# Loading z and x ahead of most weights, and preparing the weights in steps among the first tiles of z

## The chip, the core and the metric

The kernel runs on one core of one Trainium2 chip. The metric is the device time of one execution, in microseconds (us). Inputs and output lie in the chip's memory (DRAM) at the start and at the end. All arithmetic is in 32-bit floats.

## What is computed

The input `x` is one image of 128 x 256 positions (S = 128 rows, I = 256 places in a row) with C = 256 channels. Two layers follow one another, each with a residual sum:

```
x = x + L0(gn(x), z, ...)      # attention along each row, 8 heads of 32, biased by z
x = x + L1(gn(x), ...)         # attention along each row, 4 heads of 64, within a band of +-16
```

`gn` is a group norm over the whole image: 32 groups of 8 channels, each with one mean and one variance taken over all 128 x 256 positions. Nothing of layer 0 can be normalized before all of `x` has been read once.

Layer 0 turns each row `m` (256 x 256) into queries, keys and values with `Wq`, `Wk`, `Wv` after a layer norm, adds to the scores a bias `b = layer_norm(z) @ Wb.T` (one 256 x 256 matrix for each of the 8 heads, the same for all rows), takes a softmax, weighs the values, gates the result with `sigmoid(m @ Wg.T + bg)` and projects it with `Wo`. `z` is 256 x 256 x 128, so it is 33.6 MB, as large as `x`. Layer 1 projects with `w_in` (3 x 256 columns), takes the banded softmax and projects with `w_out`.

The scale and shift of the layer norms are folded into the weights on the chip before they are used: `wq`, `wk`, `wv` and `wb` are multiplied by the norm's scale, have their column means taken out (with a matrix product by `avg`, a matrix of 1/128), and the norm's shift becomes the biases `qb`, `kb`, `vb_r`, `bz_r`. A few more constants are scaled too (`w_in`, `bin_c`, `bg_c`, `wo`), and the bias of layer 1's values is carried through `w_out` into `bout_r` (with the helper tile `bv_w`). This is called the preparation below.

## The kernel before

`fast_kernel` holds the work that is timed. It has these stages.

1. **Constants.** 26 DMAs, all issued by SyncE (SP in the profile), load the weights and the small vectors (the helpers `load_chunks`, `load_col`, `load_row`, and the loops for `w_out` and `bv_c`), 2.6 MB together. The preparation stands in the text right after the pools are opened (L996 to L1040).
2. **Front.** The 16 tiles of `z` (`zjobs`, 2.1 MB each) and the 8 blocks of `x` (4.2 MB each) are read once. `z_front` loads a tile of z and takes its statistics (16 BATCH_NORM_STATS2 on VectorE, L1069); `z_back` turns the tile of the round before on TensorE (L1091), ScalarE copies it out of PSUM (L1093), and `z_project` multiplies it by `wbz`, a copy of the prepared `wb`; every second tile, a table of exponentials of the bias goes to `eb` (L1135). `x_block` loads a block of x and takes its statistics (16 BATCH_NORM_STATS2 on 512 elements, L1144).
3. **Group norm of layer 0 and first rows.** After the last block of x, `plan` spreads the moments, the loads of the first pairs of rows and their normalization over the remaining tiles of z (`mark` is called four times in each tile).
4. **Layer 0**, 64 pairs of rows, then **layer 1**, 64 pairs of rows, both ordered by hand and mostly bound by TensorE.

The order inside the front is written out by hand (`tc.manual_schedule()` keeps it). In the constants and at the boundary of the layers the framework's scheduler orders each engine. Engines run their own queues in order; a DMA is issued in the order of the queue that issues it.

The loop of the front, before:

```python
for n, job in enumerate(zjobs):
    front = z_front(*job)
    if behind is not None:
        z_back(*behind)
    behind = (*job, *front)
    if nx < nga and nx * 9 <= n * nga:
        x_block(nx)
        nx += 1
        if nx == nga:
            ended = n
    mark(4)
```

So x block 0 goes with tile 0, none goes with tile 1, and blocks 1 to 7 go with tiles 2 to 8; `ended` is 8, and `plan` counts from there. There are three buffers for tiles of z and two for blocks of x: the load of tile n + 3 waits until tile n has been turned, and the load of block j + 2 waits until the statistics of block j are done.

At the boundary of the layers, `moments_steps` finishes the second group norm and writes `M1` and `R1` (`M_l`, `R_l` in the profile, L984; POOL takes the root at L979). Then `bv_w`, `ps_bo` and the sum into `bout_r` (L1614 to L1620), the turning of `M1` and `R1` (`ps_mr`, L1628), the scaling of `w_in` by `R1c` (L1631), and the loads of layer 1's first pairs (`xt1`, L1647), which `turn` transposes (`ps_x`, L1655). The pool that holds `xt1` reuses memory that layer 0 has given back; its first loads wait for whatever used that memory last.

Of the kernel before, what the change touches and what calls it, by code (L numbers as in the profile page):

```python
# [9 lines left out]
F32 = mybir.dt.float32  # L10
AF = mybir.ActivationFunctionType
ALU = mybir.AluOpType
# [4 lines left out]
P = 128  # L17
# [756 lines left out]
def fast_kernel(  # L774
# [25 lines left out]
    nc = tc.nc  # L800
    S, I, C = x.shape
    CZ = z.shape[2]
    H = wbT.shape[1]
# [4 lines left out]
    NB = I // P  # L808
    KC = C // P
# [3 lines left out]
    QS = 1.0 / math.sqrt(D0)  # L813
    QS1 = 1.0 / math.sqrt(D1)

    const = ctx.enter_context(tc.tile_pool(name="const", bufs=1))
# [4 lines left out]
    ones = const.tile([P, P], F32, name="ones")  # L821
    nc.vector.memset(ones, 1.0)
    avg = const.tile([P, P], F32, name="avg")
    nc.vector.memset(avg, 1.0 / P)
    mhalf = const.tile([P, 64], F32, name="mhalf")
    nc.vector.memset(mhalf, -0.5)

    def load_chunks(src, n, name):
        t = const.tile([P, src.shape[0] // P, n], F32, name=name)
        nc.sync.dma_start(t, src.rearrange("(k p) n -> p k n", p=P))  # L830
        return t

    def load_col(src, name):
        t = const.tile([P, src.shape[0] // P], F32, name=name)
        nc.sync.dma_start(t, src.rearrange("(k p) -> p k", p=P))
        return t

    def load_row(src, name):
        n = src.shape[0]
        t = const.tile([P, n], F32, name=name)  # L840
        nc.sync.dma_start(t, src.unsqueeze(0).broadcast_to([P, n]))
        return t


# [63 lines left out]

    eb = const.tile([P, H, NB, I], F32, name="eb")

    wq = load_chunks(wqT, C, "wq")
    wk = load_chunks(wkT, C, "wk")
    wv = load_chunks(wvT, C, "wv")
    wg = load_chunks(wgT, C, "wg")
    wo = load_chunks(woT, C, "wo")
    w_in = load_chunks(w_inT, 3 * C, "w_in")

    w_out = const.tile([P, KC, C], F32, name="w_out")
    for a in range(KC):
        for h in range(H1):  # L920
            n = P // H1
            nc.sync.dma_start(w_out[h * n : (h + 1) * n, a, :], w_outT[(2 * h + a) * n : (2 * h + a + 1) * n, :])
    wb = const.tile([CZ, H], F32, name="wb")
    nc.sync.dma_start(wb, wbT)
    lnw_c = load_col(ln_m_w, "lnw_c")
    lnb_c = load_col(ln_m_b, "lnb_c")
    lzw_c = load_col(ln_z_w, "lzw_c")
    lzb_c = load_col(ln_z_b, "lzb_c")
    bg_c = load_col(bg, "bg_c")
    bin_c = load_col(b_in[0 : 2 * C], "bin_c")  # L930
    bo_r = load_row(bo, "bo_r")
    bv_c = const.tile([P, KC], F32, name="bv_c")
    for h in range(H1):
        n = P // H1
        nc.sync.dma_start(
            bv_c[h * n : (h + 1) * n, :],
            b_in[2 * C + h * D1 : 2 * C + (h + 1) * D1].rearrange("(a i) -> i a", i=n),
        )
    bout_r = load_row(b_out, "bout_r")

    qb = const.tile([P, KC], F32, name="qb")
    kb = const.tile([P, KC], F32, name="kb")
    vb_r = const.tile([P, C], F32, name="vb_r")
    bz_r = const.tile([P, H], F32, name="bz_r")
# [42 lines left out]
    pz = tc.alloc_tile_pool(name="pre_z", bufs=1, side="right")  # L987
# [4 lines left out]
    def mm(name):  # L992
        return ps_mm.tile([P, 512], F32, name=name, tag="mm")


    lnb_w = pz.tile([P, KC, P], F32, name="lnb_w")  # L996
    for k in range(KC):
        nc.vector.tensor_scalar_mul(lnb_w[:, k, :], ones, lnb_c[:, k : k + 1])
    for w, dst in ((wq, qb), (wk, kb)):
        for m in range(KC):  # L1000
            ps = mm("b_ps")
            for k in range(KC):
                nc.tensor.matmul(
                    ps[:, 0:1], w[:, k, m * P : (m + 1) * P], lnb_c[:, k : k + 1],
                    start=(k == 0), stop=(k == KC - 1),
                )
            nc.vector.tensor_copy(dst[:, m : m + 1], ps[:, 0:1])
    nc.vector.tensor_scalar_mul(qb, qb, QS)
    ps = mm("b_ps")
    for k in range(KC):  # L1010
        nc.tensor.matmul(ps[:, :C], lnb_w[:, k, :], wv[:, k, :], start=(k == 0), stop=(k == KC - 1))
    nc.vector.tensor_copy(vb_r, ps[:, :C])
    lzb_w = pz.tile([P, P], F32, name="lzb_w")
    nc.vector.tensor_scalar_mul(lzb_w, ones, lzb_c)
    ps = mm("b_ps")
    nc.tensor.matmul(ps[:, :H], lzb_w, wb, start=True, stop=True)
    nc.vector.tensor_copy(bz_r, ps[:, :H])

    for k in range(KC):
        nc.vector.tensor_scalar(wq[:, k, :], wq[:, k, :], lnw_c[:, k : k + 1], QS, ALU.mult, ALU.mult)  # L1020
        nc.vector.tensor_scalar_mul(wk[:, k, :], wk[:, k, :], lnw_c[:, k : k + 1])
        nc.vector.tensor_scalar_mul(wv[:, k, :], wv[:, k, :], lnw_c[:, k : k + 1])
        nc.vector.tensor_scalar_mul(w_in[:, k, 0:C], w_in[:, k, 0:C], QS1)

    for w in (wq, wk, wv):
        ps = mm("b_ps")
        for k in range(KC):
            nc.tensor.matmul(ps[:, :C], avg, w[:, k, :], start=(k == 0), stop=(k == KC - 1))
        for k in range(KC):
            nc.vector.scalar_tensor_tensor(w[:, k, :], ps[:, :C], -1.0 / KC, w[:, k, :], ALU.mult, ALU.add)  # L1030
    nc.vector.tensor_scalar_mul(wb, wb, lzw_c)
    nc.vector.tensor_scalar_mul(bin_c[:, 0:KC], bin_c[:, 0:KC], QS1)

    nc.vector.tensor_scalar_mul(bg_c, bg_c, 0.5)
    nc.vector.tensor_scalar_mul(wo.rearrange("p k n -> p (k n)"), wo.rearrange("p k n -> p (k n)"), 0.5)


    ps = mm("b_ps")
    nc.tensor.matmul(ps[:, :H], avg, wb, start=True, stop=True)
    nc.vector.tensor_sub(wb, wb, ps[:, :H])  # L1040

    nga = S // GA
    st0 = pz.tile([P, nga, G, 3], F32, name="st0")
# [5 lines left out]
    IB, IS = 32, 64  # L1049
    zjobs = [(b, i) for b in range(NB) for i in range(0, I, IB)]  # L1050
    z_rows = z.rearrange("(u t) (p b) c -> t p u (b c)", t=NB, b=NB)
    wbz = pz.tile([P, 4, 4, H], F32, name="wbz")
    nc.vector.memset(wbz, 0.0)
    for j in range(4):
        nc.vector.tensor_copy(wbz[:, j, j, :], wb)

    def z_front(b, i0):

        nonlocal zrs
        zt = pz.tile([P, IB, CZ], F32, name="zt", tag="zt", bufs=3)  # L1060
        nc.sync.dma_start(
            zt.rearrange("p (u b) c -> p u (b c)", b=NB), z_rows[b, :, i0 // NB : (i0 + IB) // NB, :]
        )

        st = pz.tile([P, IB, 3], F32, name="zst", tag="zst", bufs=2)
        for i in range(0, IB, 2):
            if i % (IB // 4) == 0 and i:
                mark(i // (IB // 4))
            nc.vector.bn_stats(  # L1069
                st[:, i : i + 2, :].rearrange("p i f -> p (i f)"),  # L1070
                zt[:, i : i + 2, :].rearrange("p i c -> p c i"),
            )
        at = i0 % IS
        if at == 0:
            zrs = pz.tile([P, IS], F32, name="zrs", tag="zrs", bufs=3)
        rs = zrs[:, at : at + IB]
        nc.vector.tensor_scalar(rs, st[:, :, 2], 1.0 / CZ, 1e-5, ALU.mult, ALU.add)
        nc.gpsimd.tensor_tensor(rs, rs, mhalf[:, :IB], ALU.pow)
        return zt, zrs
# [383 lines left out]
    ended = None  # L1463

    def mark(quarter):
        if ended is not None:
            plan.pop((n - ended, quarter), nothing)()


    behind, nx, n = None, 0, 0  # L1470
    with tc.manual_schedule():
        for n, job in enumerate(zjobs):
            front = z_front(*job)
            if behind is not None:
                z_back(*behind)
            behind = (*job, *front)
            if nx < nga and nx * 9 <= n * nga:
                x_block(nx)
                nx += 1
                if nx == nga:  # L1480
                    ended = n
            mark(4)
        assert not plan
        z_back(*behind)
        z_project()
        z_exp()
        now.project("qT", 0)
        now.project("kT", 0)
        for f in ("centre", "scale"):
            getattr(nxt, f)()  # L1490
        for r in range(2):
            nxt.moments(r)
# [8 lines left out]
    with tc.manual_schedule():  # L1501
        old = was = Nobody()
        es = nn3 = None
        for p in range(NP):
# [3 lines left out]
            ps = now.scores(0, 0)  # L1508
# [95 lines left out]
    with tc.tile_pool(name="l1", bufs=2) as sb, tc.tile_pool(  # L1604
# [4 lines left out]

        def mm1(name):  # L1610
            return ps_mm.tile([P, 512], F32, name=name, tag="mm")


        bv_w = const.tile([P, KC, P], F32, name="bv_w")  # L1614
        for k in range(KC):
            nc.vector.tensor_scalar_mul(bv_w[:, k, :], ones, bv_c[:, k : k + 1])
        ps = mm1("ps_bo")
        for k in range(KC):
            nc.tensor.matmul(ps[:, :C], bv_w[:, k, :], w_out[:, k, :], start=(k == 0), stop=(k == KC - 1))
        nc.vector.tensor_add(bout_r, bout_r, ps[:, :C])  # L1620


        nM1 = const.tile([P, KC], F32, name="nM1")
# [292 lines left out]
```

## Time and profile before

| | us |
|---|---|
| median of 5 runs (3374.55 to 3379.31) | 3375.36 |
| the profiled execution, its own time | 3375.4 |
| its span, first to last instruction (granted TensorE clock 0.982) | 3373.6 |
| first load of z issued | 17.4 |
| statistics of the last block of x begin | 155.3 |
| first scores of layer 0 | 242.6 |
| `R_l` of the second group norm written | 2119.3 |
| first transpose of layer 1 | 2123.9 |

The times below are microseconds from the start of the span. PE is TensorE, PEld its weight loads, DVE VectorE, ACT ScalarE, POOL GpSimd, SPq and ACTq the issuing of DMAs by SyncE and ScalarE. In a line of the timeline stand the start, the duration, the engine, the line of the code, the operation, what it writes and reads, how many instructions are merged, and in brackets how long the engine had been idle before and what released it. A line of the windows gives for one stretch the busy time of each engine, the granted TensorE clock, the busy share of the 16 DMA engines and what they moved.

### The profile page before, as it was taken

Reading aid. Unit: us, or ns where it says so; the run is one execution under the profiler, and the core shown is the slowest. Engines: PE = TensorE matmul, PEld = TensorE weight load, DVE = VectorE, ACT = ScalarE, POOL = GpSimd, SP = SyncE. Lnnn points to the kernel's source line nnn. Section 1 sums busy time; section 2 is a strip of 40 time slices with the busy share of each in tenths; the row PEclk is TensorE's granted clock in tenths of the full one; section 3 lists DMA queues with packets and bytes.
Section 4 is the critical chain, followed back from the end, with each engine's and each line's share of the span. In section 5 each row is a group of like instructions: output and inputs, shape, how many; then the busy total and the mean of one; then the engine's idle time right before and its main releaser. Section 6 shows DMA issues by size and latency. Waiting matters only on the chain. (4 is left out here: it accounts for less than half of the span.)

```text
span 3373.6 us, 81186 instructions
## 1 busy us (share of the span) xinstructions
PE 3226.1 (96%) x35158; PEld 2036.2 (60%) x35158; DVE 2023.4 (60%) x3218; ACT 1463.7 (43%) x2121; POOL 1974.7 (59%) x1377
## 2 busy tenths in 40 slices
PE   5389999999999999999999998899999999999998
PEld 3255555555555555555555554567767767677676
DVE  7966666666666666666666666366544444443456
ACT  2264444444444444444444443344444444444443
POOL 2378887777777777887777774333333333333332
PEclk8699999999999999999999999899999999999999
DMA  9951212221221222122212221121111211212111
GB/s 333 383 135 42 73 48 74 73 73 48 73 74 54 59 71 68 48 73 74 73 48 73 73 65 50 54 64 53 60 57 52 65 52 53 64 52 62 55 57 53
DMA packets 198814, 262.89 MB, mean 78 GB/s; under 512 B 46288, under 2 KB 147536, under 8 KB 197296
## 3 DMA queue, kind: packets, MB, share of 16 engines
q1 hardware_dynamic: 197776, 257.35, 24.9%
q8 instruction: 278, 4.55, 0.7%
q14 instruction: 88, 0.72, 0.1%
q10 hardware_dynamic: 672, 0.26, 0.0%
HBM read 188.82 MB, written 68.75 MB: 76 GB/s over the span
## 5 line engine op out<-in xcount | busy, mean ns | idle before, releaser
L1310 POOL TENSOR_TENSOR eboth<-e 128x512 f32<-128x512 f32 x512 | 640.4, 1273 | 389.7 <-DVE e L1305 386.5
L1305 DVE TENSOR_TENSOR e<-ps_sc,eb 128x1024 f32<-128x1024 f32 x512 | 602.8, 1219 | 316.2 <-ACT ps_sc L1296 225.5
L1296 ACT ACTIVATE ps_sc<-ps_sc 128x1024 f32<-128x1024 f32 x512 | 492.8, 1006 | 507.4 <-PE ps_sc L1289 507.4
L1705 POOL TENSOR_TENSOR e<-e,bw 128x384 f32<-128x384 f32 x256 | 259.8, 1038 | 443.3 <-ACT e L1703 443.3
L1666 PE MATMUL ps_p<-xgT,w_in 128*128 128x512 f32 x1024 | 467.9, 600 | 0.0
L1658 POOL TENSOR_TENSOR xt<-xt,bout_r 128x1024 f32<-128x1024 f32 x64 | 152.3, 2380 | 382.3 <-PE ps_x L1655 382.3
L1758 DVE TENSOR_TENSOR yo<-ps_y,xt 128x512 f32<-128x512 f32 x128 | 88.4, 690 | 380.8 <-PE ps_y L1754 372.5
L1666 PEld LDWEIGHTS ps_p<-xgT,w_in 128*128 128x128 f32 x1024 | 188.4, 190 | 198.9 <-issue 165.4
L1289 PE MATMUL ps_sc<-qT,kT 32*128 32x256 f32 x4096 | 293.7, 400 | 2.1 <-ACT kT L1259 2.1
L1320 PE MATMUL ps_ov<-e,v 128*32 128x256 f32 x4096 | 274.1, 385 | 0.5 <-DVE oT L1334 0.5
L1255 PE MATMUL ps_p<-xnT,wq 128*128 128x512 f32 x512 | 254.1, 618 | 0.7 <-POOL xnT L1242 0.6
L1255 PE MATMUL ps_p<-xgT,wg 128*128 128x512 f32 x512 | 253.9, 618 | 0.0
L1754 PE MATMUL ps_y<-w_out,oT 128*128 128x256 f32 x1024 | 250.3, 387 | 2.6 <-DVE oT L1739 2.6
L1362 PE MATMUL ps_y<-wo,oT 128*128 128x256 f32 x1024 | 243.9, 381 | 7.2 <-POOL oT L1352 7.2
L1362 PEld LDWEIGHTS ps_y<-wo,oT 128*128 128x128 f32 x1024 | 195.7, 191 | 88.3 <-issue 59.5
L1289 PEld LDWEIGHTS ps_sc<-qT,kT 32*128 32x128 f32 x4096 | 185.4, 184 | 94.4 <-issue 70.5
L1270 PE MATMUL ps_v<-wv,xnT 128*128 128x256 f32 x1024 | 242.1, 379 | 0.0
L1255 PE MATMUL ps_p<-xnT,wk 128*128 128x512 f32 x512 | 240.6, 592 | 0.0
L1681 PE MATMUL ps_v<-w_in,xgT 128*128 128x256 f32 x1024 | 231.8, 379 | 0.0
L1736 DVE RECIPROCAL rv<-odd 128x256 f32<-128x256 f32 x128 | 224.4, 1753 | 4.4
L1681 PEld LDWEIGHTS ps_v<-w_in,xgT 128*128 128x128 f32 x1024 | 194.4, 190 | 53.5 <-issue 30.1
L1270 PEld LDWEIGHTS ps_v<-wv,xnT 128*128 128x128 f32 x1024 | 189.6, 190 | 50.9 <-issue 31.1
(163 smaller groups left out, 4986.2 us busy)
## 6 DMA issues: line engine op xcount, KB each, us to landing
zt<-in_z_dram SPq DMA_DIRECT2D x16, 2048.0 KB
xa<-in_x_dram SPq DMA_DIRECT2D x8, 4096.0 KB
xt<-in_x_dram SPq DMA_DIRECT2D x64, 512.0 KB
rvb<-rsum SPq DMA_DIRECT2D x256, 128.0 KB
x<-xo SPq DMA_DIRECT2D x16, 2048.0 KB
xt<-x SPq DMA_DIRECT2D x64, 512.0 KB
out_dram<-yo SPq DMA_DIRECT2D x63, 512.0 KB
rs_r<-rs_d SPq DMA_DIRECT2D x63, 256.0 KB
```

Of the source, the lines that this page charges most:

```text
L1255: nc.tensor.matmul(ps, w[:, k, m * P : (m + 1) * P], getattr(self, src)[:, k, :], start=(k == 0), stop=(k == KC - 1),)
L1270: nc.tensor.matmul(self.ps_v[:, b * C : (b + 1) * C], self.xnT[:, k, t * P : (t + 1) * P], wv[:, k, :], start=(k == 0), stop=(k == KC - 1),)
L1289: nc.tensor.matmul(self.pss[q // 2][:, q % 2, b, :], self.kT[rs, c, r * I + b * P : r * I + (b + 1) * P], self.qT[rs, c, r * I : (r + 1) * I],
L1296: nc.scalar.activation(self.pss[a], self.pss[a], AF.Exp)
L1305: nc.vector.tensor_tensor(e, pss[a], eb[:, h : h + 2], ALU.mult)
L1310: nc.gpsimd.tensor_tensor(t, es[a][:, :, 0, :], es[a][:, :, 1, :], ALU.add)
L1320: nc.tensor.matmul(ov[q * D0 : (q + 1) * D0, :], self.v[:, r, b, h * D0 : (h + 1) * D0], es[q // 2][:, q % 2, b, :], start=(b == 0), stop= ...
L1362: nc.tensor.matmul(self.ps_y[:, b * C : (b + 1) * C], self.oT[r][:, k, b * P : (b + 1) * P], wo[:, k, :], start=(k == 0), stop=(k == KC - 1),)
L1666: nc.tensor.matmul(ps, w_in[:, k, n * C + m * P : n * C + (m + 1) * P], self.xgT[:, k, :], start=(k == 0), stop=(k == KC - 1),)
L1681: nc.tensor.matmul(ps[:, b * C : (b + 1) * C], self.xgT[:, k, t * P : (t + 1) * P], w_in[:, k, 2 * C : 3 * C], start=(k == 0), stop=(k == ...
L1705: nc.gpsimd.tensor_tensor(e[:, q], e[:, q], bcast(bw.rearrange("p b w -> p (b w)"), 1, KC), ALU.mult)
L1754: nc.tensor.matmul(ps[:, b * C : (b + 1) * C], self.oT[r][:, k, b * P : (b + 1) * P], w_out[:, k, :], start=(k == 0), stop=(k == KC - 1),)
```

## The change

- The helpers no longer issue DMAs. They put them on a list, `queued`, and `load(n)` issues the next n of the list from ScalarE's queue.
- The list has a new order: `lnb_c`, `wq`, `wk`, `wv`, `wb`, `lnw_c`, `lzw_c`, `lzb_c` first, then `wg`, `wo`, `w_in`, `w_out` (8 pieces), `bg_c`, `bin_c`, `bo_r`, `bv_c` (4 pieces), `bout_r`.
- The front begins with the load of z tile 0 in two halves (SyncE), the first eight of the list (ScalarE), and the load of z tile 1 (SyncE). From tile 1 on, four of the list are issued from ScalarE after the statistics of each tile, until it is empty (tile 5).
- x block 0 moves from tile 0 to tile 1 (`nx < n`); blocks 1 to 7 stay with tiles 2 to 8, and `ended` stays 8.
- The preparation becomes a generator, `weights()`, that is taken in steps: two steps after tile 0's statistics, three among those of tile 1 (`mark`), one after them, and the rest among tile 6's.
- `bv_w`, `ps_bo` and the sum into `bout_r` move from the boundary of the layers into that last part, and `bv_w` goes from the pool `const` to the pool `pz`.

```diff
+    queued = []
+
+    def load(n):
+        for _ in range(min(n, len(queued))):
+            nc.scalar.dma_start(*queued.pop(0))
+
     def load_chunks(src, n, name):
         t = const.tile([P, src.shape[0] // P, n], F32, name=name)
-        nc.sync.dma_start(t, src.rearrange("(k p) n -> p k n", p=P))
+        queued.append((t, src.rearrange("(k p) n -> p k n", p=P)))
         return t
...
+    def weights():
+        lnb_w = pz.tile([P, KC, P], F32, name="lnb_w")
+        for k in range(KC):
+            nc.vector.tensor_scalar_mul(lnb_w[:, k, :], ones, lnb_c[:, k : k + 1])
+        for w, dst in ((wq, qb), (wk, kb)):
...
+            yield
+            for m in range(KC):
+                nc.vector.tensor_copy(dst[:, m : m + 1], pss[m][:, 0:1])
...
+        nc.vector.memset(wbz, 0.0)
+        for j in range(4):
+            nc.vector.tensor_copy(wbz[:, j, j, :], wb)
+        yield
+        for k in range(KC):
+            nc.vector.tensor_scalar_mul(w_in[:, k, 0:C], w_in[:, k, 0:C], QS1)
...
+        bv_w = pz.tile([P, KC, P], F32, name="bv_w")
...
+        ps = mm("ps_bo")
+        for k in range(KC):
+            nc.tensor.matmul(ps[:, :C], bv_w[:, k, :], w_out[:, k, :], start=(k == 0), stop=(k == KC - 1))
+        yield
+        nc.vector.tensor_add(bout_r, bout_r, ps[:, :C])
...
-    def z_front(b, i0):
+    def z_load(b, i0, parts=1):
+        zt = pz.tile([P, IB, CZ], F32, name="zt", tag="zt", bufs=3)
+        for u in range(parts):
+            part = slice(u * IB // parts, (u + 1) * IB // parts)
+            nc.sync.dma_start(
+                zt[:, part].rearrange("p (u b) c -> p u (b c)", b=NB),
+                z_rows[b, :, (i0 + part.start) // NB : (i0 + part.stop) // NB, :],
+            )
+        return zt
+
+    def z_front(b, i0, zt):
...
     def mark(quarter):
+        if n == 1 and quarter < 4 or n == 6:
+            next(prepare, None)
         if ended is not None:
             plan.pop((n - ended, quarter), nothing)()
...
     behind, nx, n = None, 0, 0
+    prepare = weights()
     with tc.manual_schedule():
+        zts = [z_load(*zjobs[0], 2)]
+        load(8)
+        zts.append(z_load(*zjobs[1]))
         for n, job in enumerate(zjobs):
-            front = z_front(*job)
+            front = z_front(*job, zts.pop(0) if zts else z_load(*job))
+            if n == 0:
+                next(prepare)
+                next(prepare)
+            else:
+                load(4)
+                if n == 1:
+                    next(prepare)
             if behind is not None:
                 z_back(*behind)
             behind = (*job, *front)
-            if nx < nga and nx * 9 <= n * nga:
+            if nx < n and nx < nga:
                 x_block(nx)
...
-        bv_w = const.tile([P, KC, P], F32, name="bv_w")
-        for k in range(KC):
-            nc.vector.tensor_scalar_mul(bv_w[:, k, :], ones, bv_c[:, k : k + 1])
-        ps = mm1("ps_bo")
-        for k in range(KC):
-            nc.tensor.matmul(ps[:, :C], bv_w[:, k, :], w_out[:, k, :], start=(k == 0), stop=(k == KC - 1))
-        nc.vector.tensor_add(bout_r, bout_r, ps[:, :C])
```

## Prediction, made before the changed kernel had run

> **What bounds the kernel now.** I read the windows first, cut where the timelines show the front's stages to change (columns: stretch, length, busy us and instruction count of PE, PEld, DVE, ACT, POOL, granted clock, DMA share, GB/s).
>
> ```profile
> 0.00:17.40 17.40, 3.12 (x15) 3.12 (x15) 2.91 (x18) 1.28 (x1) 2.90 (x15) 1.00 0.50 144
> 17.40:155.30 137.90, 69.97 (x411) 47.41 (x410) 124.82 (x304) 43.38 (x91) 43.76 (x9) 0.76 1.03 389
> 155.30:165.00 9.70, 0.00 (x0) 0.00 (x0) 9.66 (x17) 0.00 (x0) 5.11 (x1) 0.50 1.09 354
> 165.00:179.00 14.00, 8.79 (x56) 6.71 (x56) 11.16 (x37) 4.64 (x9) 6.10 (x2) 0.66 0.16 55
> 179.00:224.00 45.00, 39.41 (x320) 24.98 (x313) 31.60 (x105) 34.36 (x78) 33.96 (x9) 1.00 0.93 252
> ```
>
> For 17.4 us nothing is near its limit. From 17.4 to 155.3 the DMA engines are full (1.03, 389 GB/s) and VectorE is busy 124.8 of 137.9 us: two limits side by side. Then VectorE alone finishes the last block of x; from 165 to 179 the DMA engines run empty, so what follows doesn't depend on how much they had moved before.
>
> The timeline of SyncE's queue says why the first stretch is empty:
>
> ```profile
> 0.80 0.44 SPq L830 DMA_DIRECT2D wq<-in_wqT_dram  x1
> ...
> 16.93 0.42 SPq L841 DMA_DIRECT2D bout_r<-in_b_out_dram  x1
> 17.40 0.43 SPq L1061 DMA_DIRECT2D zt<-in_z_dram  x1
> 17.88 4.25 SPq L1142 DMA_DIRECT2D xa<-in_x_dram  x1
> ```
>
> Twenty-six issues of about 0.5 us stand ahead of the first tile of z. VectorE's timeline tells which limit ends last at the other end:
>
> ```profile
> 117.78 5.41 DVE L1069 BATCH_NORM_STATS2 zst<-zt 128x6 f32<-128x256 f32 x16
> 123.22 0.18 DVE L1077 TENSOR_SCALAR zrs<-zst 128x32 f32<-128x32 f32 x1
> 123.83 9.64 DVE L1144 BATCH_NORM_STATS2 st<-xa 128x6 f32<-128x512 f32 x16 [0.42 <-DMA xa<-in_x_dram]
> ...
> 155.28 9.61 DVE L1144 BATCH_NORM_STATS2 st<-xa 128x6 f32<-128x512 f32 x16 [0.44 <-DMA xa<-in_x_dram]
> ```
>
> Blocks 5 and 7 of x wait 0.4 us for their data: DMA ends last, VectorE half a microsecond behind. Last, the timeline at the boundary of the layers:
>
> ```profile
> 2118.98 0.29 DVE L984 COPY R_l<-rs_l 128x256 f32<-128x256 f32 x1 [5.55 <-POOL rs_l L979]
> ...
> 2119.40 0.93 SPq L1647 DMA_DIRECT2D xt<-x  x2
> ...
> 2119.91 0.15 DVE L1630 COPY R1c<-ps_mr 128x1 f32<-128x1 f32 x1
> ...
> 2123.85 1.94 PE L1655 MATMUL ps_x<-ident,xt 128*128 128x128 f32 x8 [3.51 <-DMA xt<-x]
> ```
>
> Layer 1's first load is issued only after `R_l` is written, and TensorE waits 3.51 us for it. Everything else between 242.6 us and the end isn't touched by the change.
>
> **What the skill says.** The Trainium skill, "DMA: Bandwidth & Descriptors", section "Issuing engines are not separate DMA queues": DMAs from ScalarE and SyncE run on the same 16 engines and interleave; a second issuer saves only issue time. Its section "Queues, rings and completion order" adds that each engine takes turns between queues, packet by packet. The trace agrees: at 200.39 us ScalarE sends `rs_d` just after SyncE issued a tile of z at 200.25; that tile is used first at 216.32, 16.1 us later, where the one before (issued 193.01, used 202.13) took 9.1. So I let weights and z share the bandwidth, and give no bandwidth for the second queue.
>
> **Part 1: the loads.** The stream of z and x is issued from 0.8 us instead of 17.4. Before the last block of x it needs 9 x 2.097 + 8 x 4.194 = 52.4 MB; at 389 GB/s that is 134.8 us, and the trace took 137.9 from first issue to use, so start and landing cost 3.1 us. After the change the weights ride along: five of 0.262 MB, `w_in` 0.786, `w_out` 0.262, two broadcast rows of 0.131, 2.62 MB or 6.7 us. Last block ready: 0.8 + 3.1 + 55.05 MB / 389 GB/s (141.5) = **145.4**, against 155.3. Gain 9.9. The small vectors cost little: `lnb_c`, issued at 12.02, releases VectorE at 14.26, 2.2 us with its latency.
>
> The 26 issues move to ScalarE: 0.5 us each, 13 us. The first twelve stand ahead of its first copy (`zT`), before it has work; the others come four to a tile, 2 us, where ScalarE is busy 43.4 of 137.9 us. Behind them in its queue are the copies that TensorE's transposes wait for, and behind those the next loads of z; room for 2 us is there, as the tile loads are queued some 10 us before they are needed. In the program as built, DMAs share eight semaphores in turn, which adds waits: tile 1 waits until `wv` has landed, `lzb_c` until the first half of tile 0. By the shared rate, `wq`, `wk`, `wv` and as much of z (1.6 MB, 4 us) are there by about 8 us, while the second half of tile 0 flows until 11: no gap. The blocks' waits on small loads (block 1 on `w_in`, block 2 on a piece of `w_out`) end well before SyncE reaches them.
>
> **Part 2: the preparation on VectorE.** It used to lie in the empty stretch; now it lies between statistics. From the rows of the timeline: `lnb_w` 0.48, four copies 0.64, `qb` 0.16, `lzb_w` 0.28, `vb_r` and `bz_r` 0.57, six scalings 2.05, `wb` 0.22, six sums with the column means 2.28, `wb` and `wbz` 0.71: 7.4 us, 0.8 of them while tile 1 is still on its way. At tile 6: `w_in` 0.49, `bin_c` and `bg_c` 0.32, `wo` 0.43, `bv_w` 0.56, `bout_r` 0.41: 2.2 us. Is VectorE then the limit? Tile 1 lands after z0, z1, 0.79 MB of first weights and 1.3 MB of the next, 6.3 MB: 0.8 + 3.1 + 16.2 = 20.1. Its statistics (5.6) with 6.6 of preparation and about 1 us of round trips to TensorE (before, VectorE waited 1.7 and 0.8 us for the column means; now statistics fill most of that) end at 33.3. From x block 0 to block 7 the old trace took 155.28 - 37.82 = 117.5 us, 3.6 of it waiting for x; one tile of z less (5.6) and 2.2 more give 110.5. VectorE reaches block 7 at **143.8**, before the data. The cover of the 9.6 us of new work is thus thin, 1.6 us: every microsecond beyond it shows.
>
> x block 0 moves from tile 0 to tile 1: the order of the stream is z0, z1, x0, z2, x1 instead of z0, x0, z1, z2, x1; no bytes change, and `ended` stays 8. After block 7 the sequence of every engine is the old one, and the DMA engines idle inside it, so the rest of the front moves rigidly with block 7.
>
> **Part 3: the boundary.** `ps_bo` takes TensorE 2.1 us at 2113.5, beside POOL's root (5.44 us), and `bout_r` takes VectorE 0.41 us while it waits for `ps_mr` anyway: their removal brings nothing. But moving `bv_w` out of `const` shifts the buffers of `xt1`. In the changed program the first of these loads waits no longer for `R_l`; it waits for an old `rvb` load, a product of the second last pair and an old projection, and stands in SyncE's queue right behind the store of 2102.21. It is there before 2119. The next thing late is `ps_mr` (about 2120.3 on TensorE) and `R1c` (2120.06), so the transposes start near 2120.3 instead of 2123.85: **3.5**. Neither the transposes nor ScalarE's first copy wait for the last store.
>
> **Sum.** 9.9 + 3.5 = 13.4. The profiled execution took 3375.4 us (span 3373.6 and 1.8 around it), the median is 3375.36, so nothing is to be corrected: **3362.0**. About 0.2% (6.8 us) is what a measurement of this kernel can tell from no change.
>
> Bounds. Part 1 and 2: at least 6 (round trips and shared bandwidth cost VectorE 4 us more at tile 1), at most 14 (the stream at 400 GB/s, as from 80 to 120 us: 3.9 less). Part 3: from 0 to 3.8, as the load is either still late or not; a loss is excluded, because the work there only shrinks.
>
> **Rivals.**
>
> 1. *Both parts as worked out:* 3362.0, from 3358 to 3366. For it: SyncE's lines and the wait of 3.51. Chance 0.62.
> 2. *Another wait takes the load's place at the boundary*, for instance `xt1` shares the engines with the 2.1 MB store of 2102.21 and a store's landing holds a first reuse of memory: only part 1 remains, 3365.5. Against it: 17 us lie between the store and 2119. Chance 0.13.
> 3. *VectorE takes the gain:* the steps of the preparation expose TensorE's round trips and tile 1 comes late by shared bandwidth. If the preparation's 7.4 us and 4 us of waits both show in full, part 1 shrinks from 9.9 to about 3, and the total is 3369, within 0.2% of before. For it: only 1.6 us of cover. Chance 0.10.
> 4. *Slower: ScalarE's queue is held.* SyncE's issue of tile 1 took 15.03 us in the old trace (the longest of that line's sixteen durations), because it was pushed while the engines were full. If an issue from ScalarE is held as long behind SyncE's, its copies, TensorE's transposes and the next loads of z are late at each of tiles 2 to 5. About 10 us of a hold are covered (tile 4's buffer was free some 10 us before its issue at 59.98); the rest shows four times: 4 x 5 = 20 us, less 13.4: 3382. It decides from 10 + 13.4 / 4 = 13.4 us a tile. Against it: ScalarE's issue at 200.39 took 0.40 us, though SyncE wasn't seen to push then. Chance 0.06.
> 5. *The waits for data go too:* with a stream at 400 GB/s and VectorE close behind, 17.4 us come back: 3358. Chance 0.09.
>
> That the change doesn't do what it says would be a late first z after all: its issue has no wait in the program, so I give that nothing beyond case 3.
>
> Range: cases 1, 2 and 5 and most of 3, 3357 to 3369.5. Faster by over 0.2%: cases 1, 2, 5 and a little of 3, 0.86; the same 0.08; slower 0.06.
>
> **What would show it.** Right: z issued at 0.8; tile 0's statistics at 8 to 10 us, tile 1's near 20, block 0's near 33, block 7's near 145 (now 155.28), first scores near 232.7 (now 242.6); 389 GB/s from about 4 us on; the first `ps_x` about 1.4 us after `R_l` instead of 4.9. Wrong: a `zT` copy held by a DMA issue on ScalarE, VectorE waiting for `b_ps` for more than 2 us among tile 1's statistics, block 7 later than 149, or the distance from block 7 to the first scores other than 87.3 us.

## The result, and the profile after

The changed kernel takes 3369.46 us (median of 22 runs, 3367.3 to 3371.64), the kernel before 3376.44 (42 runs). The ratio is 0.998, with a 95% interval from 0.9974 to 0.9985: 7.0 us faster, where 13.4 had been predicted. The profiled executions are 5.5 us apart (spans 3368.1 and 3373.6), and this sum is what the two traces can explain:

| stretch | before | after | gain |
|---|---|---|---|
| start to the statistics of block 7 of x | 155.28 | 151.45 | +3.83 (predicted 9.9) |
| block 7 to the first `e` of layer 0 | 89.59 | 91.38 | -1.79 (predicted 0) |
| first `e` to `R_l` | 1874.11 | 1874.33 | -0.22 |
| `R_l` to the first `ps_x` of layer 1 | 4.87 | 1.19 | +3.68 (predicted 3.5) |
| first `ps_x` to the end | 1249.75 | 1249.75 | 0 |

The boundary came out as predicted, the front gave well under half, and a stretch that was called rigid was 1.8 us longer in these two executions. The timeline around `R_l` shows the first of these:

```profile
2100.87 1.87 SPq L1685 DMA_DIRECT2D xt<-x  x2
...
2117.16 0.29 DVE L990 COPY R_l<-rs_l 128x256 f32<-128x256 f32 x1 [5.55 <-POOL rs_l L985]
...
2118.35 1.94 PE L1693 MATMUL ps_x<-ident,xt 128*128 128x128 f32 x8
```

Layer 1's first load is issued 16 us ahead of `R_l` instead of 0.4 us behind it, and the bracket with the wait for `xt` is gone.

VectorE's timeline of the front (in brackets the idle time before, and what ended it):

```profile
7.90 2.74 DVE L1103 BATCH_NORM_STATS2 zst<-zt 128x6 f32<-128x256 f32 x8 [6.30 <-DMA zt<-in_z_dram]
...
23.35 1.42 DVE L1103 BATCH_NORM_STATS2 zst<-zt 128x6 f32<-128x256 f32 x4 [6.36 <-DMA zt<-in_z_dram]
...
35.13 9.75 DVE L1178 BATCH_NORM_STATS2 st<-xa 128x6 f32<-128x512 f32 x16
...
70.86 9.64 DVE L1178 BATCH_NORM_STATS2 st<-xa 128x6 f32<-128x512 f32 x16 [4.42 <-DMA xa<-in_x_dram]
...
87.22 9.60 DVE L1178 BATCH_NORM_STATS2 st<-xa 128x6 f32<-128x512 f32 x16 [1.19 <-DMA xa<-in_x_dram]
...
151.45 9.60 DVE L1178 BATCH_NORM_STATS2 st<-xa 128x6 f32<-128x512 f32 x16
```

Tile 0 is there at 7.9 us, as predicted. Tile 1 is 3.3 us later than predicted (23.35 against 20.1), blocks 2 and 3 wait 5.6 us, and block 7 starts late and without a wait. The windows say what the stream did meanwhile (last two columns: DMA share and GB/s):

```profile
44.00:48.00 4.00, 2.53 (x24) 1.87 (x24) 4.00 (x12) 1.49 (x4) 0.00 (x0) 1.00 0.86 351
48.00:52.00 4.00, 3.29 (x32) 2.23 (x28) 3.92 (x11) 2.46 (x6) 1.52 (x1) 1.00 0.18 42
52.00:56.00 4.00, 0.98 (x8) 0.07 (x8) 4.00 (x8) 0.75 (x2) 3.90 (x1) 1.00 1.04 358
```

From 48 to 52 us the engines were nearly empty: 42 GB/s. SyncE's waits name the reason (what the issue waited for: us in total, times, longest):

```profile
SPq L1176 <- DMA bv_c<-in_b_in_dram: 18.3, 1, 18.3
SPq L1090 <- DMA xa<-in_x_dram: 17.0, 1, 17.0
...
SPq L1090 <- DMA wv<-in_wvT_dram: 10.8, 1, 10.8
...
SPq L1176 <- DMA w_in<-in_w_inT_dram: 5.7, 1, 5.7
```

The same view of the kernel before, up to 250 us:

```profile
SPq L1142 <- DVE zrs L1077: 88.0, 6, 15.0
SPq L1061 <- PE ps_t L1091: 41.1, 5, 16.1
...
SPq L1184 <- DVE zrs L1077: 14.8, 1, 14.8
SPq L922 <- DMA w_in<-in_w_inT_dram: 2.4, 1, 2.4
```

A load of z (L1090) stood 17.0 us for a load of x, with which it shares no data: in the program as built, tile 3 counts on the same semaphore (the counter by which a finished load is reported) as block 1, and it was issued only at 50.57, when block 1 had landed. Tile 1 stood 10.8 us for `wv`, block 3 long for a piece of `bv_c`. In the kernel before, every wait that showed on the loads of z and x in the front was for a buffer. But waits between loads that share no data were there already, among the weights: a piece of `w_out` (L922) stood 2.4 us for `w_in`.

In the tail of the front, VectorE waits for the last two tiles of z. First the changed kernel, then the kernel before:

```profile
212.31 5.43 DVE L1103 BATCH_NORM_STATS2 zst<-zt 128x6 f32<-128x256 f32 x16 [7.88 <-DMA zt<-in_z_dram]
220.28 5.42 DVE L1103 BATCH_NORM_STATS2 zst<-zt 128x6 f32<-128x256 f32 x16 [2.33 <-DMA zt<-in_z_dram]
```
```profile
216.32 5.43 DVE L1069 BATCH_NORM_STATS2 zst<-zt 128x6 f32<-128x256 f32 x16 [7.73 <-DMA zt<-in_z_dram]
...
222.84 5.43 DVE L1069 BATCH_NORM_STATS2 zst<-zt 128x6 f32<-128x256 f32 x16 [0.86 <-DMA zt<-in_z_dram]
```

The wait of some 8 us for tile 14 was there before the change.

### The profile page after: what moved, and what is told of

Its sections match the earlier page's. It is cut to its first block, busy times and chain, and to the rows that moved or that the text cites. A ratio compares the mean times of both kernels' runs of the same rounds, so it can differ in the third digit from the quotient of the medians.

```text
span 3368.1 us, 81193 instructions
## 1 busy us (share of the span) xinstructions
PE 3219.8 (96%) x35158; PEld 2030.7 (60%) x35158; DVE 2020.8 (60%) x3218; ACT 1462.0 (43%) x2121; POOL 1973.4 (59%) x1377
```

## The experiments

The theory after the result: (a) the boundary's gain comes only from the pool that `bv_w` is taken from, which moves the addresses of the buffers; (b) the front lost to waits on **shared semaphores**, which join loads that have no data in common; (c) the tail depends on how the small send of `rs_d` falls against the last loads of z. The rivals: the work taken from the boundary is what helped there; the stream's bandwidth and VectorE would have set block 7 in any case; TensorE sets the tail.

All results in one table. Each ratio is to runs of the kernel before on the same chip. These runs differ from chip to chip: their medians are 3376.44 beside the changed kernel, 3377.24 beside e1 and e2, 3378.69 beside e3 to e6 and 3376.87 beside e7 to e10. So ratios are compared below, and medians only within one chip. The last three columns are from the one profiled execution of each.

| run | median | ratio (95% interval) | block 7 | block 7 to first `e` | `R_l` to `ps_x` |
|---|---|---|---|---|---|
| before | | | 155.28 | 89.59 | 4.87 |
| changed | 3369.46 | 0.9980 (0.9974 to 0.9985) | 151.45 | 91.38 | 1.19 |
| e1_loads_0_5 | 3367.62 | 0.9973 (0.9962 to 0.9983) | 149.61 | 91.07 | 1.18 |
| e1_loads_0_6 | 3370.57 | 0.9979 (0.9972 to 0.9986) | 151.57 | 90.79 | 1.19 |
| e2_bv_w_in_const | 3373.97 | 0.9992 (0.9983 to 1.0) | 152.04 | 91.33 | 4.77 |
| e2_before_bv_early | 3374.32 | 0.9989 (0.9981 to 0.9998) | 155.82 | 91.89 | 1.19 |
| e3_loads_gpsimd | 3370.57 | 0.9976 (0.9966 to 0.9986) | 150.38 | 92.96 | 1.18 |
| e4_all_loads_early | 3372.99 | 0.9984 (0.9976 to 0.9991) | 153.05 | 91.70 | 1.19 |
| e5_rs_d_after_tile15 | 3365.16 | 0.9958 (0.9945 to 0.9972) | 151.29 | 85.60 | 1.19 |
| e6_gpsimd_and_rs_d | 3364.13 | 0.9956 (0.9942 to 0.9969) | 150.53 | 85.49 | 1.18 |
| e7_gpsimd_all_first | 3368.63 | 0.9975 (0.9965 to 0.9985) | 148.61 | 90.93 | 1.18 |
| e8_gpsimd_first_rs_d | 3362.09 | 0.9955 (0.9942 to 0.9969) | 149.80 | 85.56 | 1.19 |
| e9_step_at_tile_12 | 3366.87 | 0.9969 (0.9957 to 0.9981) | 148.05 | 89.80 | 1.19 |
| e10_before_rs_d | 3371.42 | 0.9983 (0.9976 to 0.9990) | 154.76 | 85.26 | 4.89 |

Kernels with the same front are 0.15 to 1.2 us apart at block 7 (changed and e5: 0.16; e7 and e8: 1.19). So a difference of a microsecond there is not read as an effect.

### The boundary: one word undone, one part alone

e2_bv_w_in_const, against the changed kernel:

```diff
-        bv_w = pz.tile([P, KC, P], F32, name="bv_w")
+        bv_w = const.tile([P, KC, P], F32, name="bv_w")
```

e2_before_bv_early, against the kernel before: the first lines stand at the end of the preparation, the removed ones at the boundary.

```diff
+    bv_w = pz.tile([P, KC, P], F32, name="bv_w")
...
+    nc.vector.tensor_add(bout_r, bout_r, ps[:, :C])
...
-        bv_w = const.tile([P, KC, P], F32, name="bv_w")
...
-        nc.vector.tensor_add(bout_r, bout_r, ps[:, :C])
```

> The changed kernel with one word undone: bv_w is taken from the pool const again, its work stays among tile 6. As built, layer 1's first load then waits for R_l again. Theory 'the address decides': the first ps_x starts 4.8 us after R_l instead of 1.2, and the time is 3.7 us longer, about 3373. Rival 'the work taken from the boundary brings it': ps_x stays 1.2 us after R_l, 3369.5.

> The kernel before with only bv_w, ps_bo and the sum into bout_r moved into the preparation (pool pz), loads and front as before. As built, layer 1's first load waits no longer for R_l. Theory: ps_x starts 1.2 us after R_l, the front stays as it was (block 7 at 155.3), time 3.7 us below before, about 3372.7. Rival 'the boundary gives nothing by itself': 3376.4.

With `bv_w` in `const` again the wait is back, although the work stays away from the boundary. Its timeline:

```profile
2117.72 0.29 DVE L990 COPY R_l<-rs_l 128x256 f32<-128x256 f32 x1 [5.55 <-POOL rs_l L985]
...
2118.15 0.93 SPq L1685 DMA_DIRECT2D xt<-x  x2
...
2122.49 1.94 PE L1693 MATMUL ps_x<-ident,xt 128*128 128x128 f32 x8 [3.74 <-DMA xt<-x]
```

SyncE's issue stands 9.2 us for `R_l` again, as it stood 9.1 us in the kernel before, and `ps_x` comes 4.77 us after `R_l`. The time is 0.0012 of 3376 us, 4 us, above the changed kernel's; the two intervals just touch, so it is the traces that decide. The other way round, the kernel before with this part alone has the short distance, 1.19, and gains 0.0011, 3.7 us (3.5 predicted), though in its profiled execution the tail was 2.3 us longer. The pool decides, not the work.

### The front: other places for the small loads

e1_loads_0_5 issues no listed load after tile 1 and five after each later tile; e1_loads_0_6 has a 6 in place of the 5.

```diff
-                load(4)
+                load(0 if n == 1 else 5)
```

> The changed kernel, but no listed load after tile 1 and five after each later tile (0, 5, 5, 5, 4 instead of 4, 4, 4, 4, 3). As built, the load of z tile 3 still shares its semaphore with the load of x block 1 and so waits until block 1 has landed. Theory 'shared semaphore': the hole in the DMA traffic near 48 to 52 us and the waits of VectorE for blocks 2 and 3 (together about 5.6 us) stay; tile 1 waits only for wq and may come up to 2 us earlier; block 7 at 149.5 to 151.5, time 3367.5 to 3369.5. Rival 'VectorE and bandwidth set it anyway': the same numbers here; the pair with e1_loads_0_6 decides.

> As e1_loads_0_5, but six listed loads after each later tile (0, 6, 6, 6, 1). The only thing that this is for: as built, the semaphores fall otherwise, and z tile 3 waits for a small piece of w_out and for tile 0's transposes, no longer for block 1 of x. Theory 'shared semaphore': no hole near 50 us, block 2 and 3 wait less than 1 us together, block 7 at 145.5 to 148, time 3 to 5.5 us below e1_loads_0_5, about 3363 to 3366. Rival 'VectorE and bandwidth set it anyway': block 7 within 1 us of e1_loads_0_5, no gain.

In the first, block 7 (149.61) and the time lie in the expected range, but not for the expected reason. Tile 1 now waited for `wq` only and began at 19.47 instead of 23.35, 3.9 us earlier where up to 2 had been expected. Of these, block 7 kept 1.84. The hole near 50 us didn't stay (344 GB/s from 48 to 52 us), though tile 3 still stood 16.3 us for block 1, and blocks 2 and 3 waited 7.5 us, more than with the hole, as VectorE came to them some 4 us earlier. The second missed. Tile 3 was free of block 1, but was issued at 50.54 all the same, since the piece of `w_out` that it now waited for was itself late. SyncE's wait, and ScalarE's timeline:

```profile
SPq L1090 <- DMA w_out<-in_w_outT_dram: 20.2, 1, 20.2
```
```profile
40.23 0.32 ACTq L832 DMA_DIRECT2D w_out<-in_w_outT_dram  x1
40.26 0.62 ACT L1127 COPY zT<-ps_t 128x512 f32<-128x512 f32 x1
46.88 3.94 ACTq L832 DMA_DIRECT2D w_out<-in_w_outT_dram  x4
50.86 0.44 ACTq L832 DMA_DIRECT2D bg_c<-in_bg_dram  x1
51.39 1.56 ACT L1127 COPY zT<-ps_t 128x512 f32<-128x512 f32 x3 [10.52 <-DMA w_out<-in_w_outT_dram]
```

ScalarE's copies stand behind the issue of a piece of `w_out` for 10.5 us. The view doesn't name what that issue waited for; it went out at 46.88, just after block 1 was ready (46.53), so a small load seems to wait for a large one too. So this pair couldn't decide; it showed that moving loads about within these two queues deals the waits anew.

e3_loads_gpsimd, against the changed kernel:

```diff
-            nc.scalar.dma_start(*queued.pop(0))
+            nc.gpsimd.dma_start(*queued.pop(0))
```

e4_all_loads_early, against the changed kernel:

```diff
-                load(4)
+                load(19 if n == 1 else 5)
```

> The changed kernel with one word changed: the listed loads are issued from GpSimd's queue instead of ScalarE's, in the same places. As built, the loads of GpSimd's queue have semaphores of their own, so no load of z or x waits for a listed load or the other way round: z tile 1 has no wait, z tile 3 waits only for tile 0 (its own buffer). Theory 'shared semaphores': tile 1 at about 19.5 to 20 us, no hole near 50 us, waits of VectorE for blocks 1 to 7 under 1.5 us together, block 7 at 144 to 147, time 5 to 7.5 us under the changed kernel, 3362 to 3364.5. Rival 'bandwidth and VectorE set it anyway': waits for x of 5 us or more stay, block 7 at 149 or later, 3367 to 3369.5.

> The changed kernel with all remaining listed loads issued from ScalarE after tile 1's statistics stand in the program (19 instead of 4, in one place), which ScalarE reaches while it has nothing else to do. Semaphores are still shared, but every listed load that a load of z or x waits for is issued before 30 us, and z tile 3 no longer waits for block 1. Tile 1 still waits for wv, so it comes at 23.4 as in the changed kernel. Theory 'shared semaphores': the hole near 50 us goes, and the 5.6 us of waits for blocks 2 and 3 with it, block 7 at 146 to 148.5, time 3364 to 3366.5. Rival 'bandwidth and VectorE set it anyway': block 7 at 150 or later, 3368 to 3370.

In the program as built, loads from GpSimd's queue have semaphores of their own. SyncE's waits up to 145 us in e3:

```profile
SPq L1176 <- DVE bt L1158: 29.4, 2, 15.7
SPq L1176 <- DVE zrs L1111: 28.0, 2, 14.8
SPq L1176 <- DVE bv_w L1066: 13.5, 1, 13.5
SPq L1090 <- PE ps_t L1125: 10.5, 2, 7.4
SPq L1176 <- DVE st L1178: 5.6, 1, 5.6
```

No wait for another load is left; all are for buffers. Tile 1 began at 19.22, the hole was gone (349 GB/s from 48 to 52 us), and block 4 began at 99.53 instead of 103.03. Bandwidth is not what GpSimd's queue should bring: the Trainium skill, "DMA: Bandwidth & Descriptors", section "Issuing engines are not separate DMA queues", says that the same 16 engines carry the loads of every issuer. What these runs show to have changed is what waits for what, and when the small loads go out. But block 7 came at 150.38, blocks 1 to 4 still waited 6.6 us with no hole in the stream, and the ratio is 0.9976, which makes 3368 us of 3376.44: all three are what the rival had forecast, not the theory. The 3.5 us gained at block 4 shrank to 1.1 at block 7, because tile 6 lost 3.0 us to two waits, where the changed kernel lost 0.64:

```profile
113.00 0.48 DVE L1066 TENSOR_SCALAR bv_w<-ones,bv_c 128x128 f32<-128x128 f32 x2 [1.67 <-issue]
...
116.11 0.42 DVE L1071 TENSOR_TENSOR bout_r<-bout_r,ps_bo 128x256 f32<-128x256 f32 x1 [1.31 <-DMA bout_r<-in_b_out_dram]
```

`bv_c` and `bout_r` are last on the list; GpSimd issued the last of them only from 103.84 us on, behind its 5.45 us of work on `zrs`.

In e4 the expectation that all small loads would be issued before 30 us was wrong: the last, `bout_r`, went out at 35.62, and tile 2 of z waited 13.4 us for `bg_c` until 35.44. Its windows show the hole in a new place:

```profile
32.00:36.00 4.00, 4.00 (x21) 3.20 (x19) 3.52 (x12) 0.00 (x0) 0.62 (x1) 1.00 0.58 159
36.00:40.00 4.00, 2.15 (x19) 1.70 (x17) 3.96 (x12) 3.90 (x7) 4.00 (x1) 1.00 0.78 180
```

Block 7 came at 153.05, and the time was the worst of the front's variants. With a hole of its own, e4 doesn't decide between the theory and the rival.

### How much is left in the front

e7_gpsimd_all_first, against e3:

```diff
-        load(8)
+        load(27)
```

e9_step_at_tile_12, against e8, which is e7 with the edit of e5 (below):

```diff
-        if n == 1 and quarter < 4 or n == 6:
+        if n == 1 and quarter < 4 or n == 12:
```

> As e3_loads_gpsimd, but all 27 listed loads are issued from GpSimd at the start, not in groups. In e3 tile 6 lost 3.0 us of VectorE because bv_c and bout_r, the last of the list, came late. Theory 'two limits in turn' (the stream of 390 GB/s sets the blocks up to 4, at 16.2 us for a tile and a block; from there VectorE, which needs 15.6, is only just ahead and shows nearly all of tile 6's preparation): blocks 1 to 4 still wait some 9 us for their data, block 4 at 99 to 101, block 7 at 147 to 149, time 2 to 3 us under e3. Rival 'only the shared semaphores were in the way': block 7 at 144 to 146. Rival 'VectorE sets all': block 7 at 150 or later.

> As e8_gpsimd_first_rs_d, with the last steps of the preparation (w_in, bin_c, bg_c, wo, bv_w, bout_r: 2.2 us of VectorE) among the statistics of tile 12 instead of tile 6, behind block 7, where VectorE waits anyway. Theory 'two limits in turn': the stream has only some tenths of a us less than VectorE at block 7, so block 7 comes 0 to 1 us earlier than in e8, and the time is within 1 us of it. Rival 'VectorE sets block 7': it comes 2.2 us earlier, at about 145.8, and the time falls by 2 us.

In e7 tile 6 has its operands, and block 7 comes at 148.61, inside the range of "two limits in turn"; e8, with the same front, has 149.80, outside it. Blocks 1 to 4 waited 2.4 us in e7, not 9, since tile 1 itself was later (23.68). The 2 to 3 us that it was to gain over e3 did not show in the times (ratios 0.9975 and 0.9976). In e9 the step of 2.2 us is gone from tile 6, and now the stream ends last again:

```profile
116.73 9.63 DVE L1178 BATCH_NORM_STATS2 st<-xa 128x6 f32<-128x512 f32 x16 [1.85 <-DMA xa<-in_x_dram]
...
148.05 9.61 DVE L1178 BATCH_NORM_STATS2 st<-xa 128x6 f32<-128x512 f32 x16 [0.34 <-DMA xa<-in_x_dram]
```

Block 7 gains 1.75 us over e8, from which e9 differs by this edit alone, and 0.56 over e7, which has e8's front. So the gain alone doesn't decide between the theory's 0 to 1 us and the rival's 2.2; the waits of blocks 5 and 7 do show that VectorE is no longer last. The step cost more at its new place: the distance from block 7 to the first `e` went from 85.56 to 89.80, and the kernel lost 4.8 us against e8, where a difference within 1 us had been expected. I had called VectorE free there, because it waits there. In the trace of e9, TensorE stands 3.4 us at `ps_bo` for `bv_w`, ScalarE's copies `zT` then wait up to 5.3 us for TensorE, the load of a tile of z stands 11.2 us for the turning (6.8 in e8), and from 196 to 200 us the stream falls to 33 GB/s (296 in e8). So the step held up the chain that frees the buffers of z.

### The tail: the send of `rs_d`

e5_rs_d_after_tile15, against the changed kernel; e10_before_rs_d is the same edit on the kernel before.

```diff
-        (5, 3): lambda: now.send(nc.scalar),
...
-        (7, 2): lambda: now.fetch(nc.scalar),
+        (7, 1): lambda: now.send(),
+        (7, 2): lambda: now.fetch(),
```

> The changed kernel with the first send of rs_d (512 elements of 4 bytes, scattered in DRAM) taken from ScalarE's queue at tile 13 to SyncE's queue behind the load of z tile 15, and its fetch to SyncE's queue too. Theory 'the send slows the loads of z beside it': the slow stretch (204 to 210 us at 17 to 77 GB/s) moves behind tile 15, tile 14 waits under 1.5 us instead of 7.9, and the distance from block 7 to the first e shrinks from 91.4 by 3 to 5.6 us (then TensorE's turning is the limit), time 3364 to 3367. Rival 'tile 14 is late for another reason' or 'TensorE sets the tail anyway': distance within 1 us of 91.4, time 3368.5 to 3370.

> The kernel before with only the send of rs_d moved behind tile 15's load, as in e5. Theory 'the send slows the loads of z beside it, in both kernels': block 7 at 155.3 as before, the first e 85.5 us after it instead of 89.6, time 4 us under before. Rival 'only the changed kernel suffers from it': no gain.

The send writes 512 elements of 4 bytes to DRAM. In the changed kernel it is issued from ScalarE at 196.42, half a microsecond behind the load of tile 14 (195.86). The windows of the changed kernel:

```profile
202.00:204.00 2.00, 2.00 (x18) 0.90 (x17) 1.97 (x9) 1.74 (x4) 0.36 (x2) 1.00 1.72 73
204.00:206.00 2.00, 2.00 (x20) 1.74 (x24) 0.42 (x3) 1.34 (x3) 2.00 (x1) 1.00 0.58 17
206.00:208.00 2.00, 2.00 (x18) 1.16 (x17) 0.00 (x0) 2.00 (x7) 2.00 (x1) 1.00 0.94 71
208.00:210.00 2.00, 0.86 (x8) 0.59 (x6) 0.00 (x0) 2.00 (x7) 1.11 (x1) 1.00 1.12 63
```

The DMA engines count as busy and move little, and from 204 us on VectorE (third of the busy columns) runs out of work. With the send behind tile 15 on SyncE's queue (e5), the windows from 206 to 210 us, then SyncE's and VectorE's timelines:

```profile
206.00:208.00 2.00, 2.00 (x18) 0.90 (x16) 2.00 (x7) 2.00 (x6) 2.00 (x1) 1.00 1.02 340
208.00:210.00 2.00, 1.49 (x16) 1.25 (x12) 2.00 (x7) 2.00 (x8) 2.00 (x1) 1.00 1.10 369
```
```profile
204.51 1.56 SPq L1252 DMA_DIRECT2D rs_d<-lrs  x1
218.10 0.33 SPq L1257 DMA_DIRECT2D rs_r<-rs_d  x1
```
```profile
205.68 5.41 DVE L1103 BATCH_NORM_STATS2 zst<-zt 128x6 f32<-128x256 f32 x16
...
236.89 2.35 DVE L1339 TENSOR_TENSOR e<-ps_sc,eb 128x1024 f32<-128x1024 f32 x2 [4.11 <-ACT ps_sc L1330]
```

Tile 14 waits no more, and the first `e` comes 85.60 us after block 7: 5.8 us less than in the changed kernel, just above the 3 to 5.6 that were expected. The kernel before gains as well: 89.59 became 85.26 (its first `e` is the line below), and 0.0017 of its time.

```profile
240.02 2.36 DVE L1305 TENSOR_TENSOR e<-ps_sc,eb 128x1024 f32<-128x1024 f32 x2 [4.16 <-ACT ps_sc L1296]
```

The Trainium skill's "DMA: Bandwidth & Descriptors", section "Queues, rings and completion order", has the engines take turns between queues; put behind the load in the load's own queue, the send no longer comes between its packets, and these runs agree. They show that the send, at its old place in ScalarE's queue, slows the loads beside it. Its queue and its time were moved together, so which of the two counts is not shown, nor why 2 KB do so much.

### The best version

> Both edits together, of e3_loads_gpsimd and e5_rs_d_after_tile15. If both theories hold the gains add up: first e at about 230 to 235 instead of 242.8, time 3357 to 3361. If only one holds, 3362 to 3367.

> e7_gpsimd_all_first and the send of rs_d behind tile 15's load together. If the front and the tail are independent, block 7 as in e7 (about 148) and the first e 85.5 us later, at 233.5; time 2 to 3 us under e6, about 0.9948 of the kernel before.

Both edits together bring 0.9956 and 0.9955, which can't be told from e5 alone (0.9958, 0.9945 to 0.9972). So the gain of the tail is there, and none of the front's variants shows beside it. The median of e6 is 3 us above the range for "both", 2.3 of them from the slower chip, and inside the range for "only one". Of e8, block 7 came at 149.80 and not 148; its ratio of 0.9955 can't be told from the 0.9948 that was expected. e8 beats both kernels: the changed one is at 0.9980 with an interval from 0.9974 on, and e8's interval ends at 0.9969.

## Why the prediction was right at the boundary and wrong in the front

**Part 3, the boundary: right.** 3.5 predicted, 3.68 in the trace, 4 and 3.7 in the two runs of e2, by the named mechanism. The rival "another wait takes the load's place" is out.

**Part 1, the loads: the step that failed.** The term that failed is the stream's: 55.05 MB at 389 GB/s without a gap, 141.5 us. That z is issued at 0.8 and tile 0 comes at 8 was right (27 issues stood ahead of z in the trace before, not 26; the 17.4 us stay). "389 GB/s from about 4 us on", "no gap", and "the blocks' waits on small loads end well before SyncE reaches them" were wrong: from 4 to 16 us the stream ran at 278 to 333 GB/s, and from 48 to 52 us at 42. I had the list of waits, reckoned that the one on `wv` ends by about 8 us (SyncE stood for it until 12.7), and waved the others through. I did not follow the wait of tile 3 on block 1 at all, because a load of x is no small load. The prediction knew that loads share semaphores; the error was not to follow each of these waits to its end.

What this cost is read at block 3, the last that waits for data. By the prediction's own sum, block 3 (29.9 MB) is there at 0.8 + 3.1 + 76.8 = 80.7 us; it began at 87.22, 6.5 us later. From there VectorE runs to block 7 in 64.2 us without a wait for data. That length is the same in every variant of the changed kernel in which it has no such wait and no late operand on the way (64.2 to 64.4, in both e1, e2_bv_w_in_const, e4, e5, e7 and e8 too), and the prediction's figures for VectorE give 64.1. So what was late at block 3 stayed late: block 7 came at 151.45 instead of 145.4, 6.05 us.

Not all of it comes from shared semaphores. The hole from 48 to 52 us is worth some 3.6 us (an estimate: 347 GB/s less than 389 for 4 us). Where no load of z or x waits for a listed one, block 3 began at 83.24 (e3), 84.26 (e7) and 85.56 (e8, with e7's front): 1.7 to 4.0 us earlier than in the changed kernel, and still 2.5 to 4.9 later than 80.7. These runs move the small loads too, so the share is a rough one, and the times don't resolve it: e3 and e7 are at 0.9976 and 0.9975 where the changed kernel is at 0.9980. For the rest, e3's stream was slow at the start as well, 279 to 342 GB/s from 4 to 16 us; why is not shown.

**Part 2: the cost was right, the cover was not.** The preparation cost VectorE what was listed; its round trips to TensorE were 0.50 and 0.45 us at tile 1 and 0.64 at tile 6. But the cover of 1.6 us was read at block 7 only. Stepped through block by block with the prediction's own figures, data and VectorE meet to within half a microsecond at blocks 2 to 4, at 64.5, 80.7 and 96.9 us (an estimate), so there was no cover there: a load that is late at one of these blocks makes everything behind it late. With the same figures block 7 still comes at 145.5, so it is not the later of two sums that misled, but the stream's term in it.

**"The rest of the front moves rigidly": not so.** The distance to the first scores was to be 87.3 and was 89.1. It lies between 89.6 and 93.0 (to the first `e`) in every kernel that sends `rs_d` beside tile 14, and between 85.3 and 85.6 where the send stands behind tile 15 and nothing else is in the way. With the tail of the kernel before, e2_before_bv_early has 91.9, so whether the change itself lengthened the tail is not shown; the tail varies by that much from one profiled execution to another. I had cited the slow load of tile 14 and used it only as a sign that bandwidth is shared, though 2 KB beside 2.1 MB can't cost 7 us by their bytes. It was the larger gain.

**The rivals.** The time, 3369.46, lies at the very end of the stated range, which rival 3 had stretched to 3369.5; that it lies inside is luck. It is near rival 3's time, but not by its mechanism: VectorE was late because its data was. Rival 3's own sum doesn't come out either: 7.4 and 4 us less 1.6 of cover leave nothing of the 9.9, not 3, and the 143.8 holds 6.6 of the 7.4 already. And the upper bounds with a stream at 400 GB/s (14 us, and rival 5) pass over VectorE's 143.8, which allows 11.5. Rival 4, a held queue of ScalarE, cost the changed kernel one wait of 2.5 us; in e1_loads_0_6 it was 10.5.

## What to carry to other kernels

When a change reorders DMAs, write down for each large load every wait that the built program gives it, with the time at which that wait ends, and treat a wait on a load of another queue as a dependency. Where two limits run side by side, step both through block by block, to see where there is no cover: here it was at blocks 2 to 4, and the cover at the end was of no use to them. And a stall that is cited as evidence should be priced as a gain: the same 8 us wait stood in the profile before, its removal was worth more (4.3 and 5.8 us in the two kernels) than the front's whole gain of 3.8, and it had nothing to do with the change.

## What was not expected of the hardware

A DRAM write of 2 KB in pieces of 4 bytes was expensive. Elsewhere in the changed kernel an issue stood 7.8 us for such a send (`rs_d`, SyncE's waits); in e5 it was issued at 204.51 and the fetch behind it at 218.10, with no bytes counted from 212 to 218 us and a DMA share of 0.00, so it takes some 6 us after the last load has landed. The Trainium skill, "Perfetto Trace Analysis", section "DMA Instruction — HWDGE (DVE, Sync)", says that the completion of a DMA waits for its writes to be confirmed, and that this "can cause a surprisingly long delay especially when the write target is HBM". The 6 us without traffic agree with that; that it holds up other queues' loads, 17 to 73 GB/s from 202 to 210 us, it does not say. An issue of a DMA stands in GpSimd's own row for 0.5 to 0.9 us in e3; one from ScalarE takes its queue 0.32 to 0.66 us in the changed kernel, and its copies can run beside it (an issue at 37.17, a copy at 37.22).
